# Issuing a batch's load one block later in a two-layer attention kernel

## The chip, the cores and the metric

The kernel runs on one core of a Trainium2 chip. The metric is the device time of one execution in microseconds (us), as a median of several runs. Each core has TensorE (PE in the profile; its weight loads are PEld), VectorE (DVE), ScalarE (ACT), GpSimd (POOL) and SyncE (SP). SyncE here only issues DMAs.

## The reference

The input x is 16 batches of 256 channels by 32 x 32 positions, in float32. Two layers are applied, each of the form x = x + attention(gn(x)):

```
def _L0_conv_ref(x, Wq, bq, Wk, bk, Wv, bv, rel_h, rel_w):
    ...                                   # b = 16, heads = 4, d = 64, n = 1024
    q = proj(Wq, bq)
    k = proj(Wk, bk)
    v = proj(Wv, bv)
    sim = jnp.einsum('bhdi,bhdj->bhij', q, k)
    rel = (rel_h + rel_w).reshape(heads, d, n)
    qpos = jnp.einsum('hdi,bhdj->bhij', rel, q)
    attn = jax.nn.softmax(sim + qpos, axis=-1)
    out = jnp.einsum('bhdn,bhmn->bhdm', v, attn)

x = x + _L0_conv_ref(_gn(x), ...)
x = x + _L1_conv_ref(_gn(x), ...)
```

`_gn` takes, for each batch, the mean and variance over all channels, all rows and a group of two columns (16 groups), and normalizes with them.

## The kernel before, in words

A *unit* is one batch in one layer: `units` holds 32 pairs (b, l) in the order (0,0), (1,0), (2,0), (0,1), (3,0), (1,1), (4,0), (2,1) and so on, so that from unit 3 on the odd units are second layers and the even ones first layers, until the batches run out. A unit has four *blocks*: a pair of heads (pr = 0 or 1) by a half of the 512 query positions (half = 0 or 1). Block b = 0..3 of unit u is (u, b // 2, b % 2). The loop `for n in range(len(blocks)): block(n)` (L712) writes out all 128 blocks, and the order of the code is the order of the instructions on each engine. Engines meet only by semaphores.

In a block, for each of eight stretches j of 128 key positions, VectorE writes the position term into PSUM (`seed`, L332), TensorE adds the product of k and q to it (`scores`, L348), ScalarE takes the exponential into a tile p (L357), and VectorE adds the p's up for the denominators (`add_up`, L366 and L368). TensorE then multiplies p with v (`attend`, L382). Between these stand the projections of the next heads or the next unit (`project` L251, `values` L281, `positions` L309), and the group norm of units further ahead: sums of x by ScalarE (L176) for unit u + 2 start near the end of block 0 of unit u, `norm_squares` follows in block 2, `norm_apply` (L231) one unit later.

The denominators take a way over DRAM. After each second block (half = 1) TensorE sums the p's over the partitions (`sums_of_p`, L405), and ScalarE copies products and sums out of PSUM to the tile od (`take_out`, L422). Then four small DMAs bring the sums into `den_all` (L431). In the next block (half = 0) `reciprocals` takes 1/x on VectorE (L439), writes it to DRAM (rd, two DMAs, L442) and reads it back, broadcast over 64 partitions (rden, two DMAs of 256 KB, L445). At the end of that block `finish` multiplies with it (L456), adds bias and x (L457), and in the second layer writes the result out (L459, 512 KB):

```
for h in range(2):
    nc.sync.dma_start(
        rdens[u, pr][h * D : (h + 1) * D],
        rd[h : h + 1].to_broadcast([D, 2, HALF]),
    )
```

After finish VectorE still has an `add_up` and the seeds for j = 1, 2, 3 of the next block before it, and then, in that next block, the last additions of the block before and the seed for j = 4.

All these DMAs are issued by SyncE, and so are the loads of x (L101, two DMAs of 512 KB for a batch). The first three batches are loaded ahead of the loop, the other 13 in it, by `load_x`, during unit u for the batch of unit u + 3:

```
def load_x(b):
    xt[b] = xpool.tile([P, CC, N], F32, tag="x", name=f"x_{b}")
    for cc in range(CC):
        nc.sync.dma_start(xt[b][:, cc, :], flat(x[b, cc * P : (cc + 1) * P]))
```

`units[u + 3][0] not in xt` is true in the odd units 1, 3, ..., 25. The pool of x has five tiles, used in turn.

Of the kernel before, what the change touches and what calls it, by code (L numbers as in the profile page):

```python
# [52 lines left out]
def fast_path(ctx, tc, sh, x, layers, out, W, den_all, token):  # L53
# [42 lines left out]
    xt = {}  # L96
# [5 lines that stand above are left out]
# [26 lines left out]
    units = [(b, 0) for b in range(3)]  # L128
# [3 lines left out]
    NU = len(units)  # L132
# [47 lines left out]
    def norm_sums(u, gs):  # L180
        if u not in reds:
            reds[u] = small.tile([P, G], F32, tag="red", name=f"red_{u}")
        for g in gs:
            of_group(u, g, AF.Identity, reds[u])
# [26 lines left out]
    def norm_squares(u, gs):  # L211
        for g in gs:
            of_group(u, g, AF.Square, sums[u], bias=negs[u][:, g : g + 1])
# [14 lines left out]
    def norm_apply(u, gs):  # L228
        rstd, shift = rss[u]
        for g in gs:  # L230
            nc.scalar.activation(  # L231
                grouped(xns[u], g),
                grouped(xt[units[u][0]], g),
                AF.Identity,
                bias=shift[:, g : g + 1],
                scale=rstd[:, g : g + 1],
            )
# [89 lines left out]
    def seed(blk, j, tag):  # L327

        u, pr, half = blk
        ps = psum2(tag, f"ps_{u}_{pr}_{half}_{j}")  # L330
        ab = abt[u, pr][:, :, j, :]
        nc.vector.tensor_tensor(  # L332
            ps.rearrange("p h (w y) -> p h w y", y=H),
            ab[:, :, :H].unsqueeze(2).to_broadcast([P, 2, XH, H]),
            ab[:, :, H + half * XH : H + (half + 1) * XH]
            .unsqueeze(3)
            .to_broadcast([P, 2, XH, H]),
            ALU.add,
        )
        seeds[blk, j] = ps  # L340

    def scores(blk, j):
        u, pr, half = blk
        ps = seeds.pop((blk, j))
        for h, hs in enumerate(QUARTERS):
            for x, c in enumerate(QUARTERS):
                j0 = j * P + x * D
                nc.tensor.matmul(  # L348
                    ps[c, h, :],
                    ks[u, pr][hs, j0 : j0 + D],  # L350
                    qs[u, pr][hs, half * HALF : (half + 1) * HALF],
                    start=False,
                    stop=True,
                    skip_group_check=True,
                )
        p = ppool.tile([P, 2, HALF], F32, tag="p", name=f"p_{u}_{pr}_{half}_{j}")
        nc.scalar.activation(p, ps, AF.Exp, bias=W.shift)  # L357
        probs[blk, j] = p

    def add_up(blk, j):  # L360
        u, pr, half = blk
        if j == 0:
            return
        if j == 1:
            accs[blk] = apool.tile([P, 2, HALF], F32, tag="acc", name=f"acc_{u}_{pr}_{half}")
            nc.vector.tensor_tensor(accs[blk], probs[blk, 0], probs[blk, 1], ALU.add)  # L366
        else:
            nc.vector.tensor_tensor(accs[blk], accs[blk], probs[blk, j], ALU.add)  # L368
# [66 lines left out]
    def reciprocals(u, pr):  # L435

        n = index[u, pr, 0]
        r8 = fpool.tile([P, 2, 8], F32, tag="r8", name=f"r8_{u}_{pr}")
        nc.vector.reciprocal(r8, den_all[:, n : n + 2, :])  # L439
        rd = dpool.tile([2, 2, HALF], F32, tag="rd", name=f"rd_{u}_{pr}")  # L440
        for x in range(2):
            nc.sync.dma_start(rd[:, x, :].rearrange("h (a b) -> h a b", b=8), r8[:, x, :])  # L442
        rdens[u, pr] = opool.tile([P, 2, HALF], F32, tag="rden", name=f"rden_{u}_{pr}")
# [5 lines that stand above are left out]
# [23 lines left out]
    def prepare(u, b):  # L472

        x, y = ring[3], ring[2]
        if b == 0:
            return (
                values(u, 1, psum2(x, f"pv_{u}_1")),
                project(u, 1, "q", psum2(y, f"pq_{u}_1")),
            )
        if b == 1:  # L480
            return (
                project(u, 1, "k", psum2(x, f"pk_{u}_1")),
                positions(u, 1, psum2(y, f"pa_{u}_1")),
            )
        u += 1
        if u == NU:
            return (nothing, nothing), (nothing, nothing)
        if b == 2:
            return (
                project(u, 0, "q", psum2(x, f"pq_{u}_0")),  # L490
                project(u, 0, "k", psum2(y, f"pk_{u}_0")),
            )
        return (
            values(u, 0, psum2(x, f"pv_{u}_0")),
            positions(u, 0, psum2(y, f"pa_{u}_0")),
        )

    def block(n):
        blk = blocks[n]
        u, b = divmod(n, BPU)  # L500
        half = blk[2]
        before = blocks[n - 2][:2] if half == 0 and n > 0 else None
        after = blocks[n + 1] if n + 1 < len(blocks) else None
        one, two = u + 1 < NU, u + 2 < NU

        pieces = u + 1 < NU or b < 2
        f0, f1, f2, f3 = ring

        if half == 1:
            add_up(blocks[n - 1], 7)  # L510
        for j in range(1, 4):
            scores(blk, j)
        if b == 2 and u + 3 < NU and units[u + 3][0] not in xt:
            load_x(units[u + 3][0])
        (first, first_out), (second, second_out) = prepare(u, b)
        first(0)
        if b == 0 and one:
            norm_apply(u + 1, range(0, 1))
        if b == 1 and two:
            norm_sums(u + 2, range(9, 11))  # L520
        seed(blk, 4, f1)
        scores(blk, 4)
        add_up(blk, 1)
        if half == 0:
            if before:
                reciprocals(*before)
            add_up(blk, 2)
        if b == 0 and one:
            norm_apply(u + 1, range(1, 5))
        if b == 1 and two:  # L530
            norm_sums(u + 2, range(11, 12))
        if b == 2 and two:
            norm_squares(u + 2, range(0, 5))
        second(0)
        if half == 1:
            second_out()
        first(1)
        first_out()
        seed(blk, 5, f0)
        scores(blk, 5)  # L540
        if half == 0:
            add_up(blk, 3)
            second(1)
            second_out()
        seed(blk, 6, f1)
        scores(blk, 6)
        if pieces and half == 0:
            ring[2:] = f3, f2
        seed(blk, 7, ring[2])
        scores(blk, 7)  # L550
        if half == 1:
            add_up(blk, 2)
            add_up(blk, 3)
        add_up(blk, 4)

        if after:
            seed(after, 0, f0)
        if before:
            finish(*before)
        if b == 0 and one:  # L560
            norm_apply(u + 1, range(5, 9))
        if b == 0 and two:
            norm_sums(u + 2, range(0, 2))
        if b == 1 and two:
            norm_sums(u + 2, range(12, G))
        if b == 1 and one:
            norm_apply(u + 1, range(9, 11))
        if b == 2 and two:
            norm_squares(u + 2, range(5, 11))
        po = psum2(ring[3], f"po_{n}")  # L570
        values_of_p = attend(blk, po)
        values_of_p(0)
        if two and half == 1:
            mean, mean_out = (norm_mean if b == 1 else norm_var)(u + 2, zeroed(f1, f"pm_{n}"))
            mean(0)
        if after:
            scores(after, 0)
        if two and half == 1:
            mean(1)
            values_of_p.word()  # L580
            mean_out()
        add_up(blk, 5)
        if half == 1:
            add_up(blk, 6)
            add_up(blk, 7)
        if after:
            for j in range(1, 4):
                seed(after, j, ring[j % 3])
        if half == 0:
            add_up(blk, 6)  # L590
        if b == 0 and two:
            norm_sums(u + 2, range(2, 9))
        if b == 1 and one:
            norm_apply(u + 1, range(11, G))
        if b == 2 and two:
            norm_squares(u + 2, range(11, G))
        values_of_p(1)
        if half == 1:
            sums_of_p(blocks[n - 1 : n + 1], po)
        take_out(blk, po)  # L600
# [410 lines left out]
```

## Time and profile before

| | |
|---|---|
| median of 3 runs | 2654.65 us (2654.4 to 2658.43) |
| profiled execution | 2655.58 us |
| its span, first to last instruction | 2652.5 us |
| granted clock of TensorE, mean | 0.995 |
| busy: TensorE, VectorE, ScalarE, GpSimd | 98%, 91%, 75%, 7% of the span |
| DMA: moved, mean rate | 75.48 MB, 28 GB/s |
| largest kinds of DMA | rden 128 x 256 KB, x 32 x 512 KB, output 32 x 512 KB |

A profile's row of a group reads: line, engine, operation, output<-inputs, count, and times. A timeline's row gives the start in us from the span's beginning, the duration, engine and line, what it writes and reads, how many instructions were merged, and in brackets how long the engine had been idle before it and what ended that. An arrow in the waits points from the one who waited to the one who released it. For DMAs the row tells of the issue on SyncE's queue (SPq), not of the transfer.

### The profile page before, as it was taken

The numbers are of one execution on the slowest core, as the hardware profiler recorded it, in microseconds if no ns is written. First come the engines' busy times: TensorE is split into PE (matmuls) and PEld (weight loads), VectorE is DVE, ScalarE is ACT, GpSimd is POOL, SyncE is SP. The second block draws the span as 40 slices with busy tenths as digits, with TensorE's granted clock in tenths as the row PEclk, the third lists the DMA queues.
The fourth block names the chain that finished last, engine by engine and source line by source line (L and its number), as shares of the span: only waits on it lengthen the run. The fifth ranks groups of instructions, "written<-read, shape, count | busy, mean of one in ns | idle before, by whom it ended". The sixth has DMA issues, their size and how long they took to land.

```text
span 2652.5 us, 86141 instructions
## 1 busy us (share of the span) xinstructions
PE 2591.0 (98%) x38406; PEld 1389.7 (52%) x38406; DVE 2423.2 (91%) x2198; ACT 1980.2 (75%) x3916; POOL 176.5 (7%) x450
## 2 busy tenths in 40 slices
PE   7999999999999999999999999999999999999994
PEld 3555555555555555555555555555555555555552
DVE  6999999999999999999999999999999999999996
ACT  5778777787777787777877777877778777778652
POOL 1000000000000000000000000000000000000000
PEclk9999999999999999999999999999999999999997
DMA  2010010101001010010100101001010100000001
GB/s 74 11 33 18 26 34 19 34 26 34 26 19 42 18 42 18 18 50 10 42 26 10 50 18 34 26 26 34 19 34 27 34 26 19 26 18 26 26 26 34
DMA packets 61499, 75.48 MB, mean 28 GB/s; under 512 B 43200, under 2 KB 44736, under 8 KB 61120
## 3 DMA queue, kind: packets, MB, share of 16 engines
q1 hardware_dynamic: 59664, 69.83, 9.1%
q8 instruction: 302, 4.95, 0.8%
q14 instruction: 77, 0.63, 0.1%
q10 hardware_dynamic: 1456, 0.07, 0.0%
HBM read 52.04 MB, written 17.30 MB: 26 GB/s over the span
## 4 chain that ended last, share of the span: by engine, by line
PE 84%; DVE 6%; DMA 6%; SPq 2%; issue 1%; ACT 1%; POOL 0%; DVEq 0%; POOLq 0%
PE po L382 30%; PE ps L348 29%; PE pv L281 7%; PE pq L251 7%; PE pk L251 7%; DVE ps L332 3%; PE po L405 2%; DMA rd<-r 2%; DMA rden<-rd 2%; PE pa L309 2%; DVE acc L368 2%; DMA den_all<-od 1%; SPq L431 1%; DVE x L457 1%; DVE od L456 1%
## 5 line engine op out<-in xcount | busy, mean ns | idle before, releaser
L357 ACT ACTIVATE p<-ps,shift 128x1024 f32<-128x1024 f32 x1024 | 1092.3, 1114 | 337.4 <-PE ps L348 215.4
L332 DVE TENSOR_TENSOR ps<-abt 128x1024 f32<-128x1024 f32 x1024 | 1228.7, 1228 | 112.3 <-ACT p L357 94.1
L348 PE MATMUL ps<-q,k 64*64 64x512 f32 x8192 | 997.5, 593 | 15.5 <-DVE ps L332 15.1
L368 DVE TENSOR_TENSOR acc<-acc,p 128x1024 f32<-128x1024 f32 x768 | 933.7, 1216 | 16.1 <-DVE r L439 0.2
L382 PE MATMUL po<-p,v 64*64 64x256 f32 x16384 | 933.1, 376 | 0.3 <-POOL token L152 0.3
L382 PEld LDWEIGHTS po<-p,v 64*64 64x64 f32 x16384 | 668.3, 133 | 294.6 <-issue 60.4
L348 PEld LDWEIGHTS ps<-q,k 64*64 64x64 f32 x8192 | 299.1, 133 | 443.3 <-issue 273.3
L251 PE MATMUL pq<-xn,Wq 64*64 64x512 f32 x2048 | 244.3, 592 | 4.0 <-DVE xn L640 4.0
L281 PE MATMUL pv<-Wv,xn 64*64 64x256 f32 x4096 | 244.3, 376 | 1.6 <-POOL token L152 1.3
L251 PE MATMUL pk<-xn,Wk 64*64 64x512 f32 x2048 | 242.8, 589 | 0.0
L231 ACT ACTIVATE xn<-x,nshift,rstd 128x128 f32<-128x128 f32 x501 | 213.4, 501 | 1.6 <-POOL nshift L654 1.6
L281 PEld LDWEIGHTS pv<-Wv,xn 64*64 64x64 f32 x4096 | 153.6, 133 | 103.3 <-issue 51.1
L176 ACT ACTIVATE junk<-x,neg 128x128 f32<-128x128 f32 x489 | 191.7, 399 | 0.0
L152 POOL MEMSET token<- 1x1 f32 x380 | 33.8, 89 | 2360.2 <-PE po L382 657.9
L422 ACT COPY od<-po 128x1024 f32<-128x1024 f32 x64 | 64.8, 1012 | 152.1 <-PE po L405 152.1
L366 DVE TENSOR_TENSOR acc<-p,p 128x1024 f32<-128x1024 f32 x128 | 155.9, 1218 | 0.0
L251 PEld LDWEIGHTS pq<-xn,Wq 64*64 64x64 f32 x2048 | 78.5, 134 | 145.6 <-issue 133.0
L176 ACT ACTIVATE junk<-x 128x128 f32<-128x128 f32 x480 | 144.9, 311 | 0.7 <-DVE x L457 0.7
L251 PEld LDWEIGHTS pk<-xn,Wk 64*64 64x64 f32 x2048 | 75.4, 133 | 124.2 <-issue 124.2
L220 POOL TENSOR_TENSOR rstd<-var,mhalf 128x16 f32<-128x16 f32 x30 | 113.2, 3773 | 59.1 <-ACT var L218 59.1
L456 DVE TENSOR_TENSOR od<-od,rden 128x1024 f32<-128x1024 f32 x64 | 78.2, 1221 | 31.9 <-DMA rden<-rd 31.8
L291 ACT COPY v<-pv 128x1024 f32<-128x1024 f32 x64 | 64.8, 1012 | 48.1 <-PE pv L281 48.1
(59 smaller groups left out, 921.1 us busy)
## 6 DMA issues: line engine op xcount, KB each, us to landing
rden<-rd SPq DMA_DIRECT2D x128, 256.0 KB
x<-in_x_dram SPq DMA_DIRECT2D x32, 512.0 KB
out_dram<-x SPq DMA_DIRECT2D x32, 512.0 KB
den_all<-od SPq DMA_DIRECT2D x256, 2.0 KB
rd<-r SPq DMA_DIRECT2D x128, 4.0 KB
raw<-in_L_conv_Wq_dram SPq DMA_DIRECT2D x2, 256.0 KB
raw<-in_L_conv_Wk_dram SPq DMA_DIRECT2D x2, 256.0 KB
raw<-in_L_conv_Wv_dram SPq DMA_DIRECT2D x2, 256.0 KB
```

The source lines that it names most:

```text
L176: nc.scalar.activation(junk, grouped(xt[units[u][0]], g), func, accum_out=into[:, g : g + 1], **bias)
L220: nc.gpsimd.tensor_tensor(rstd, var, W.mhalf[:, :G], ALU.pow)
L231: nc.scalar.activation(grouped(xns[u], g), grouped(xt[units[u][0]], g), AF.Identity, bias=shift[:, g : g + 1], scale=rstd[:, g : g + 1],)
L251: yield nc.tensor.matmul(pk[c, nh, :], w[l][rs, cc, c0 : c0 + D], xns[u][rs, cc, nh * HALF : (nh + 1) * HALF], start=(t == 0 and cc == 0), ...
L281: yield nc.tensor.matmul(pv[c, a, i, :], xns[u][rs, cc, j0 : j0 + D], W.wv[l][rs, cc, :], start=(t == 0 and cc == 0 and i == 0), stop=(t = ...
L332: nc.vector.tensor_tensor(ps.rearrange("p h (w y) -> p h w y", y=H), ab[:, :, :H].unsqueeze(2).to_broadcast([P, 2, XH, H]), ab[:, :, H + h ...
L348: nc.tensor.matmul(ps[c, h, :], ks[u, pr][hs, j0 : j0 + D], qs[u, pr][hs, half * HALF : (half + 1) * HALF], start=False, stop=True, skip_g ...
L357: nc.scalar.activation(p, ps, AF.Exp, bias=W.shift)
L366: nc.vector.tensor_tensor(accs[blk], probs[blk, 0], probs[blk, 1], ALU.add)
L368: nc.vector.tensor_tensor(accs[blk], accs[blk], probs[blk, j], ALU.add)
L382: yield nc.tensor.matmul(po[c, a, :QUART], vts[u][rs, j, c0 : c0 + D], p[rs, h, a * QUART : (a + 1) * QUART], start=(t == 0 and j == 0), s ...
L456: nc.vector.tensor_tensor(o, o, rden, ALU.mult)
```

## The change

The condition under which `load_x` is called in `block` names block 3 in place of block 2. The call stands at the same place in the block: behind the scores for j = 1, 2, 3, ahead of the projections.

```
         for j in range(1, 4):
             scores(blk, j)
-        if b == 2 and u + 3 < NU and units[u + 3][0] not in xt:
+        if b == 3 and u + 3 < NU and units[u + 3][0] not in xt:
             load_x(units[u + 3][0])
```

In block 2 that place lies ahead of the call of `reciprocals` (L526) and of `finish` (L559), both of which are made in blocks 0 and 2; in block 3 neither is called.

More of the change, by code (lines that the diff above doesn't have):

```diff
@@ L512, in block @@
             scores(blk, j)
-        if b == 2 and u + 3 < NU and units[u + 3][0] not in xt:
+        if b == 3 and u + 3 < NU and units[u + 3][0] not in xt:
             load_x(units[u + 3][0])
```

## Prediction

> **What bounds the kernel now.** I read the page first, for the busy shares and the chain that ended last, then the waits, and then the timelines of single engines in three stretches of two blocks.
>
> ```profile
> span 2652.5 us, 86141 instructions
> PE 2591.0 (98%) x38406; PEld 1389.7 (52%) x38406; DVE 2423.2 (91%) x2198; ACT 1980.2 (75%) x3916; POOL 176.5 (7%) x450
> PE 84%; DVE 6%; DMA 6%; SPq 2%; issue 1%; ACT 1%; POOL 0%; DVEq 0%; POOLq 0%
> ```
>
> TensorE sets the time. A change that only moves a transfer can gain no more than TensorE now loses around it. But the chain has 6% of DMA in it, so somewhere the path runs through transfers. The waits say which one (waiting engine and line, releaser: total us, times, longest):
>
> ```profile
> DVE od L456 <- DMA rden<-rd: 31.8, 19, 7.8
> PE ps L348 <- DVE ps L332: 15.1, 19, 2.7
> ```
>
> VectorE waits in finish (L456) for the broadcast reciprocals, and TensorE waits for a seed that VectorE writes (L332), as often. The 7.8 us is the last finish of the program, behind which nothing is left to do; 24.0 us lie in the other 18. SyncE's timeline (start, duration) shows what goes ahead of the reciprocals. First blocks 2 and 3 of unit 3, which has a load; then the same blocks of unit 27, which also writes its output (L459) but has no load:
>
> ```profile
> 324.61 2.43 SPq L431 DMA_DIRECT2D den_all<-od  x4
> 327.07 1.07 SPq L101 DMA_DIRECT2D x<-in_x_dram  x2
> 328.62 1.12 SPq L442 DMA_DIRECT2D rd<-r  x2
> 333.80 1.14 SPq L445 DMA_DIRECT2D rden<-rd  x2
> 341.29 0.34 SPq L459 DMA_DIRECT2D out_dram<-x  x1
> ```
>
> ```profile
> 2267.37 2.42 SPq L431 DMA_DIRECT2D den_all<-od  x4
> 2271.36 1.12 SPq L442 DMA_DIRECT2D rd<-r  x2
> 2274.42 1.14 SPq L445 DMA_DIRECT2D rden<-rd  x2
> 2282.21 0.34 SPq L459 DMA_DIRECT2D out_dram<-x  x1
> ```
>
> From issue of rd to issue of rden (which waits for rd to land) it is 333.80 - 328.62 = 5.18 us with a load and 2274.42 - 2271.36 = 3.06 without. Over all pairs of blocks I find 4.95 to 5.56 in the 13 with a load, and a mean of 3.06 in the others. The load's packets of 4 KB run from 1.2 to 4.8 us after its issue, and the small packets of rd end 0.4 to 0.8 us later: rd queues behind 1 MB. VectorE's timelines, unit 3 and then unit 27:
>
> ```profile
> 338.71 1.23 DVE L456 TENSOR_TENSOR od<-od,rden 128x1024 f32<-128x1024 f32 x1 [1.75 <-DMA rden<-rd]
> ```
>
> ```profile
> 2279.64 1.22 DVE L456 TENSOR_TENSOR od<-od,rden 128x1024 f32<-128x1024 f32 x1
> ```
>
> And ScalarE's copy L422 ends every second block, so its starts are the clock of a pair of blocks (unit 3, unit 27):
>
> ```profile
> 323.57 1.01 ACT L422 COPY od<-po 128x1024 f32<-128x1024 f32 x1 [1.34 <-PE po L405]
> ...
> 364.72 1.01 ACT L422 COPY od<-po 128x1024 f32<-128x1024 f32 x1 [3.23 <-PE po L405]
> ```
>
> ```profile
> 2266.33 1.01 ACT L422 COPY od<-po 128x1024 f32<-128x1024 f32 x1 [1.34 <-PE po L405]
> ...
> 2306.46 1.01 ACT L422 COPY od<-po 128x1024 f32<-128x1024 f32 x1 [3.23 <-PE po L405]
> ```
>
> With the load the pair takes 364.72 - 323.57 = 41.15 us, without it 40.13. Finish starts 338.71 - 323.57 = 15.14 us after the copy, against 2279.64 - 2266.33 = 13.31. So 1.83 us of delay on VectorE became 1.02 us on the path: 0.8 us was slack. TensorE's timeline shows where it bites, at the scores for the fourth block's j = 4:
>
> ```profile
> 349.39 1.09 PE L348 MATMUL ps<-q,k 64*64 64x512 f32 x8 [0.72 <-DVE ps L332]
> ```
>
> **The change, step by step.** Nothing is added or taken out. Two DMA instructions on SyncE's queue (512 KB each) move, 13 times, past four others, rd, rd, rden, rden, and in 12 of the 13 also past the output's write (L459), whose unit is of the second layer. ScalarE, VectorE, TensorE and GpSimd keep their order.
>
> *What goes away.* All 13 pairs have the pattern above. Their lengths over 40.13 are, in order of time, 0.93, 1.02, 1.22, 0.70, 1.00, 0.72, 1.51, 1.25, 1.10, 1.55, 1.44, 0.96 and 1.06 us: 14.46 us in sum. From unit 2 to unit 29 the same blocks of units without a load take 40.13 each (one 40.17), the other pairs (blocks 0 and 1) 40.25 or 40.26, also right after a load, so nothing of the loss is caught up later. In each of the 13 the excess is the start of finish less 14.1 us, within 0.03: 14.1 is the point from which TensorE feels it. Without the load ahead of it rd lands 2.04 us sooner (5.10 - 3.06, the two means), and finish, now at 15.24 in the mean, falls back to 13.2, where VectorE's own work holds it. The other pairs from unit 2 on start finish between 13.2 and 14.02 us, with one at 14.45 near the end, since den_all sometimes lands up to 1.6 us late; that stays. So I take the whole 14.46 us. What is late next is TensorE itself: the load-free pair is 40.13 us of work with no wait in its matmuls.
>
> *Where the load goes.* SyncE runs ahead of the blocks: it issues what its own waits let through. The load, which waits for nothing (SyncE's waits name no instruction of L101), will go out right behind L459, some 16 us after the copy (17.7 now, less the delay of finish), in unit 1 right behind rden. It lands some 6 us after that (1.2 us to start, the output's packets of 1.5 us ahead of it, 3.6 us of its own), so about 23 us after the copy. Behind it on the queue stand the four den_all of the next copy, 41 us after this one: 18 us free. The tile's slot was left by the write of a unit whose last finish lies six blocks back, 120 us.
>
> *What it could cost there.* First its reader: the sums of x at L176 start in the next unit's first block, for unit 3's load at 380.62, which is 57 us after the copy, so 34 us of lead remain of 49 (the load now lands 3.5 + 4.8 us after the copy). [...] By the rows, early issue is what costs 1.11 us a load, and the lead left is over five times what the load takes; I go by the rows. Secondly, in unit 1 only, the load starts on the heels of rden (256 KB twice). The nearest row is the load on the heels of den_all now: the reciprocal behind den_all starts 5.01 us after the copy with a load and 5.08 without, so no loss, and no gain to be had there either. I take 0; at worst rden is late by the load's 3.6 us, and finish at 13.0 + 3.6 passes the 14.1 by 2.5 us, once. Thirdly, 1.5 MB in a row (output and load) replaces 1.5 MB nearly in a row (load and rden) some 12 us earlier, for the other users of the DMA engines, the instruction fetches. I take 0 and keep 0 to 0.2 us a load. A gain beyond 14.46 would have to come from the pair falling below 40.13, which no load-free pair does.
>
> **Sum.** The profiled execution took 2655.58 us (span 2652.5), 0.93 above the median and inside the three runs: 2655.58 - 14.46 = 2641.1, span 2638.0. On the median: 2654.65 - 14.46 = 2640.2 us, 0.54% faster.
>
> **Rivals.** *No change* (0.05): the load pairs are long for what the load does to the core while it lands, not for its place, or the finish isn't what TensorE waits for. Then they stay at 41.24 and the time at 2654.65. For it: TensorE's named wait is only 15.1 us in all. Against: the 0.03 us fit with the start of finish.
>
> *Half* (0.07): the load behind the output disturbs something in the fourth block, at some 0.5 us a load; 14.46 - 13 x 0.5 = 8.0 us gained, 2646.7. VectorE has the least room there, 0.8 us. Against: between finish and the next den_all no compute instruction waits for a transfer.
>
> *Slower* (0.04): instruction fetches. The page has 302 of them, 16 KB each, so one every 2652 / 302 = 8.8 us, and in the fourth block one may stand behind output and load for up to 6 us. It decides from the point where TensorE stands still for more than 1.11 us a load; [...] a fetch would fall into 6 / 8.8 of the 13 loads and wait 3 us in the mean: 13 x 0.68 x 3 = 27 us, so 2640.2 + 27 = 2667. Against: in the 13 load trains of now, 7 fetches fall within 6 us of the load's issue; they take 0.9 to 1.8 us against a median of 1.0, with no loss beyond finish's. [...]
>
> **How the numbers follow.** The likeliest case, the loss gone with up to 2.5 + 2.6 us of the unknown costs and a run's scatter of some 2 us, has 0.84: 2638 to 2646. That holds 8 in 10, and the range stays there. Within 0.2% (5.3 us) is about what a measurement of this kernel can tell from no change. Faster by more: the likeliest and the half, 0.91; within: 0.05; slower: 0.04.
>
> **What would show it.** Right: rd to rden 3.1 us in all pairs, L101 after L459 on SyncE, VectorE's wait at L456 down from 31.8 to about 9 us, all pairs of blocks 2 and 3 at 40.13, DMA gone from the chain in the middle. Wrong: finish at 13.3 and pairs still over 40.13, with a new releaser at L348; L176 waiting for x; rden late in unit 1.

## The result, and the profile after

The changed kernel took 2646.12 us (median of 6 runs, 2643.18 to 2647.72), the kernel before 2656.38 us (6 runs, 2653.53 to 2660.8): a ratio of 0.9958, 95% interval 0.9945 to 0.9971. The forecast was 2640.2 us and a ratio of 0.9946. Direction and mechanism came as forecast; the gain in the medians is 10.3 us in place of 14.5.

The page of the changed kernel, span, busy shares and the chain by engine:

```profile
span 2643.5 us, 86127 instructions
PE 2589.6 (98%) x38406; PEld 1394.9 (53%) x38406; DVE 2422.9 (92%) x2198; ACT 1979.9 (75%) x3916; POOL 175.3 (7%) x450
PE 96%; issue 1%; DVE 1%; DMA 1%; POOL 0%; ACT 0%; SPq 0%; DVEq 0%; POOLq 0%
```

TensorE does the same work, but the path that ended last is now 96% TensorE (84% before), and the transfers have gone from it (1%, before 6%). The two waits that the prediction named (total us, times, longest):

```profile
DVE od L456 <- DMA rden<-rd: 8.5, 4, 7.6
PE ps L348 <- DVE ps L332: 7.1, 7, 2.7
```

7.6 of the 8.5 us are the last finish of the program; in the loop 0.9 us is left of the 24.0. SyncE's timeline for blocks 2 and 3 of unit 3, the stretch shown for before:

```profile
326.04 2.41 SPq L431 DMA_DIRECT2D den_all<-od  x4
330.02 1.12 SPq L442 DMA_DIRECT2D rd<-r  x2
333.07 1.14 SPq L445 DMA_DIRECT2D rden<-rd  x2
340.87 0.35 SPq L459 DMA_DIRECT2D out_dram<-x  x1
341.27 1.26 SPq L101 DMA_DIRECT2D x<-in_x_dram  x2
```

From rd to rden it is now 333.07 - 330.02 = 3.05 us (5.18 before), and the load goes out right behind the output, 16.3 us after the copy L422, though the block in whose code it stands begins later. In VectorE's timeline the bracket behind finish is gone, and in ScalarE's the copies that bound the pair of blocks are 40.13 us apart (41.15 before):

```profile
338.31 1.22 DVE L456 TENSOR_TENSOR od<-od,rden 128x1024 f32<-128x1024 f32 x1
```

```profile
325.00 1.01 ACT L422 COPY od<-po 128x1024 f32<-128x1024 f32 x1 [1.33 <-PE po L405]
...
365.13 1.01 ACT L422 COPY od<-po 128x1024 f32<-128x1024 f32 x1 [3.23 <-PE po L405]
```

All 13 pairs together have 0.07 us of excess over 40.13, where before had 14.46. So 14.4 us went, and yet the spans differ by 2652.5 - 2643.5 = 9.0 only. The rest was lost again in three places, found by comparing the starts of the same copies in the two profiles: 2.4 us up to the first copy (83.75 in place of 81.36), 1.2 us in the pairs without a load, and 1.9 us in the last pair of blocks (39.67 in place of 37.81).

In the last pair it is TensorE's clock, granted at 0.50 and 0.52 in the stretches below. The rows are a stretch of before and then of after; the columns are the stretch, its length, busy us (and instructions) of TensorE, weight loads, VectorE, ScalarE and GpSimd, granted clock, DMA share, GB/s:

```profile
2595.00:2598.00 3.00, 2.71 (x16) 0.31 (x9) 3.00 (x4) 1.11 (x1) 0.00 (x0) 0.50 0.39 111
```

```profile
2585.00:2592.00 7.00, 5.85 (x44) 2.44 (x48) 6.96 (x7) 3.34 (x3) 0.00 (x0) 0.52 0.29 77
```

In the 5 us ahead of these stretches TensorE is busy for only 1.5 and 2.2, as there is no next unit to project, and then its granted clock stands at half: for 3.41 us in the profile of before and for 6.83 us, twice as long, in that of after, by the clock's records. At half rate, by my estimate, the 3.41 us more are worth up to 3.41 / 2 = 1.7 of the 1.9 us. What sets these lengths was not shown. At the start TensorE was slow for longer too, in projections in whose rows no wait stands; before, then after:

```profile
28.14 1.89 PE L251 MATMUL pk<-xn,Wk 64*64 64x512 f32 x16
```

```profile
29.38 3.05 PE L251 MATMUL pk<-xn,Wk 64*64 64x512 f32 x16
```

The same 16 matmuls take 3.05 in place of 1.89 us; in block 2 of unit 3 of before, at full clock, they take 1.90. The clock's records begin, at full, at 27.91 us in the profile of before and at 31.70 in that of after; of the time ahead of that they say nothing. If the rate was half up to there, the second row lost (31.70 - 29.38) / 2 = 1.16 us, and 3.05 - 1.16 = 1.89. The same working holds in all 14 profiles of this document: in each the first copy comes 54.95 or 54.96 us after the start of the first projection plus half of the time from that start to the first record. By this estimate 1.4 of the 2.4 us at the start are half rate: (31.70 - 25.91) / 2 - (27.91 - 24.90) / 2. The other 1.0 us is the first projection itself, which began at 25.91 us and not at 24.90; ahead of it, in the profile of after, TensorE waited 0.54 us for the weights Wv.

In the pairs without a load, the cause stands in two rows of the worst one, which is one of blocks 0 and 1:

```profile
773.45 0.25 DVE L439 RECIPROCAL r<-den_all 128x16 f32<-128x16 f32 x1 [1.85 <-DMA den_all<-od]
```

```profile
775.97 1.09 PE L348 MATMUL ps<-q,k 64*64 64x512 f32 x8 [0.21 <-DVE ps L332]
```

den_all landed late, the reciprocal held VectorE's queue, and TensorE waited for the seed behind it (0.21 us stand as idle, the pair lost 0.44). None of the three places lies in code that the change touches. Whether they are the change's doing or chance was the first question for the experiments.

### The profile page after: what moved, and what is told of

It reads as the page before. It is cut to its first block, busy times and chain, and to the rows that moved or that the text cites. A ratio compares the mean times of both kernels' runs of the same rounds, so it can differ in the third digit from the quotient of the medians.

```text
span 2643.5 us, 86127 instructions
## 1 busy us (share of the span) xinstructions
PE 2589.6 (98%) x38406; PEld 1394.9 (53%) x38406; DVE 2422.9 (92%) x2198; ACT 1979.9 (75%) x3916; POOL 175.3 (7%) x450
## 4 chain that ended last, share of the span: by engine, by line
PE 96%; issue 1%; DVE 1%; DMA 1%; POOL 0%; ACT 0%; SPq 0%; DVEq 0%; POOLq 0%
PE po L382 34%; PE ps L348 33%; PE pk L251 8%; PE pv L281 8%; PE pq L251 8%; PE po L405 2%; PE pa L309 2%; PE pm L196 0%; DMA den_all<-od 0%; DVE ps L332 0%; SPq L431 0%; POOL rstd L652 0%; DVE acc L368 0%; ACT od L422 0%; DMA rden<-rd 0%
## 5 line engine op out<-in xcount | busy, mean ns | idle before, releaser
L422 ACT COPY od<-po 128x1024 f32<-128x1024 f32 x64 | 64.8, 1012 | 152.2 <-PE po L405 152.2
L262 ACT ACTIVATE q<-pq,bq 128x1024 f32<-128x1024 f32 x64 | 71.4, 1116 | 39.4 <-PE pq L251 39.4
```

The lines of the kernel that those rows point to most:

```text
L262: nc.scalar.activation(t.rearrange("p (a n) -> p a n", a=NH), pk, AF.Identity, bias=bias[l][:, pr : pr + 1])
```

## The experiments

**Is it chance?** Each kernel once more, unaltered. First the changed one:

> The changed kernel once more, unaltered, for more executions and a second profile. Theory A (the load ahead of rd cost 14.4 us and nothing replaces it; the first comparison came out smaller, 10.3 us, since 2.4 us at the start and 1.9 us at the end of the profiled execution came from TensorE's half clock lasting longer, and 1.1 us from den_all landing late by chance): the pairs of blocks 2 and 3 are 40.13 us again, start and end differ from the first profile by some us, and the medians differ by 10 to 15 us. Theory B (the new place costs some 0.3 us a load): the median gain stays at 10 us and the same pairs are over 40.13 or 40.25 as in the first profile.

Measured: 2644.49 us against 2657.18 for before in the same series, ratio 0.9954 (0.9941 to 0.9968), 12.7 us. In its profile the 13 pairs have 0.10 us of excess, the start is 82.69, the last pair 37.79, with a granted clock of 0.99, 0.50 and 0.97 in the 5, 3 and 5 us from 2578 on, so some 3.4 us at half. Then the kernel before:

> The kernel before, unaltered, for a second profile. Theory A (the first profile of before was a favourable one: start 81.36 us to the first copy L422, 0.16 us of excess outside the load pairs, one half-clock window of 3.41 us ahead of the end): the load pairs lose 14.4 us again, within 1 us, while start, the other pairs and the end are some 2 us worse in sum, as in the profiles of the changed kernel. Theory B (the changed kernel itself has the worse start, end and other pairs): the second profile of before repeats 81.4, 0.2 and one window.

Measured: 2659.63 us, ratio to the earlier runs of before 1.0003 (0.9994 to 1.0011). Its second profile has 12.73 us of excess in the load pairs (under the 13.4 that theory A allowed), a start of 83.73, a last pair of 39.61 with 6.83 us of half clock, and 0.8 us of excess in the other pairs: in sum start, end and other pairs are 4.8 us worse than in its first profile, where theory A had some 2. So the slow end belongs to neither kernel: each showed both forms. The slow start doesn't belong to the changed one either: 81.36 and 83.73 before, 83.75 and 82.69 after, and 82.31 to 83.93 in the other ten profiles. The 81.36 of the first profile, from which the forecast was made, came only once. Over both profiles of each, the spans differ by (2652.5 + 2655.5) / 2 - (2643.5 + 2640.6) / 2 = 12.0 us. For the excess outside the load pairs theory A holds less well: 0.2 and 0.8 us before, 1.3 and 1.5 us after. That stays open.

**Does the new place cost anything?** A second load behind each one, into a tile that nothing reads:

```
+    def load_more(b):
+        more = xpool.tile([P, CC, N], F32, tag="more", name=f"more_{b}", bufs=1)
+        for cc in range(CC):
+            nc.sync.dma_start(more[:, cc, :], flat(x[b, cc * P : (cc + 1) * P]))
...
             load_x(units[u + 3][0])
+            load_more(units[u + 3][0])
```

> The changed kernel, and behind each of the 13 loads in block 3 a second load of 1 MB into a tile that nothing reads. Theory A (the new place is free, 18 us of room): no difference from the changed kernel, 2644 to 2648. Theory B (a cost of 0.3 us a load in the new place, by instruction fetches or by what the load does while it lands): 4 us more than the changed kernel, 2650.

Measured: 2645.07 us, ratio 0.9952 (0.9938 to 0.9965), against 2644.49 of the changed kernel in the same series. SyncE's queue and ScalarE's copies around unit 3's load:

```profile
339.74 0.35 SPq L464 DMA_DIRECT2D out_dram<-x  x1
340.14 1.26 SPq L101 DMA_DIRECT2D x<-in_x_dram  x2
341.45 0.94 SPq L106 DMA_DIRECT2D more<-in_x_dram  x2
365.04 1.14 SPq L436 DMA_DIRECT2D den_all<-od  x2
```

```profile
323.87 1.01 ACT L427 COPY od<-po 128x1024 f32<-128x1024 f32 x1 [1.33 <-PE po L410]
...
364.00 1.01 ACT L427 COPY od<-po 128x1024 f32<-128x1024 f32 x1 [3.22 <-PE po L410]
```

40.13 us with 2 MB there, and no excess in the sum of the 13 pairs. Theory B (0.3 us a load) falls: the new place is free.

**The same doubling in the old place**, by the same edit in the kernel before:

> The kernel before, and behind each of the 13 loads in block 2 a second load of 1 MB into a tile that nothing reads: 2 MB ahead of rd. Theory A (rd queues behind the load's bytes; the excess of a pair is the start of finish less 14.1 us): rd to rden 5.1 + about 3 us, finish at 18 to 19 us, 4 to 4.8 us of excess a pair, 40 to 48 us more than before, some 2697 to 2705. Rival (the load slows the core while it lands): the excess doubles at most, 2657 + 14 = 2671.

Measured: 2697.09 us, 37.5 over before (2659.59), ratio 1.0143 (1.0127 to 1.0158). SyncE's queue and finish in unit 3:

```profile
333.04 1.06 SPq L101 DMA_DIRECT2D x<-in_x_dram  x2
334.14 0.91 SPq L106 DMA_DIRECT2D more<-in_x_dram  x2
335.15 1.81 SPq L447 DMA_DIRECT2D rd<-r  x2
342.05 1.16 SPq L450 DMA_DIRECT2D rden<-rd  x2
```

```profile
346.82 1.22 DVE L461 TENSOR_TENSOR od<-od,rden 128x1024 f32<-128x1024 f32 x1 [3.89 <-DMA rden<-rd]
```

rd to rden takes 342.05 - 335.15 = 6.9 us, in the mean of the 13 pairs too, and finish starts at 17.97 in the mean. The rule "excess is the start of finish less 14.1" gives 13 x 3.87 = 50.3 us for these pairs; they have 50.66. The absolute time fell into theory A's range; the difference from before, 37.5, stayed just under its 40 to 48, since rd went out later behind the added issues (6.21 us after the copy in the mean, 5.29 before) and so waited for less. The rival's doubling, 14 us, is far off. The same second load cost 50.66 - 14.46 = 36 us in one place and nothing in the other.

**Half of the bytes** ahead of rd:

```
-        if b == 2 and u + 3 < NU and units[u + 3][0] not in xt:
-            load_x(units[u + 3][0])
+        if b == 2 and u + 3 < NU and units[u + 3][0] not in xt:
+            load_x(units[u + 3][0], [0])
+            rest.append(units[u + 3][0])
+        if b == 3 and rest:
+            load_x(rest.pop(), [1])
```

> The load in halves: the first DMA of 512 KB in block 2 ahead of rd, the second in block 3. Theory A (a threshold: 0.9 us of slack between 13.2 and 14.1): 512 KB take 1.8 us of DMA time and delay rd by some 0.2 us, so no loss but where den_all is late; as the changed kernel, 2644 to 2648. Rival (loss in proportion to the bytes ahead of rd): half of the loss stays, 7 us, about 2652.

Measured: 2645.26 us, ratio 0.9946 (0.9932 to 0.9959). A threshold, then: 512 KB cost nearly nothing. The size of the delay was off: rd to rden is 3.89 us in the mean, 0.83 over the free case and not 0.2. Finish comes at 13.99, just inside the slack, and 1.55 of the 1.59 us of excess lie in two pairs where den_all was late as well.

**Is it block 2, or the place in the queue?** Load in block 2, but behind the reciprocals (the call in block 3 is gone):

```
             if before:
                 reciprocals(*before)
+                if b == 2 and u + 3 < NU and units[u + 3][0] not in xt:
+                    load_x(units[u + 3][0])
```

> Load in block 2 as before, but called behind the reciprocals, so behind rd and rden on SyncE's queue. Theory A (only the place ahead of rd counts): rd to rden 3.1 us, finish at 13.2 to 14.1, time as the changed kernel within 3 us, some 2644 to 2648. Rival (a load anywhere in block 2 disturbs it, or on the heels of rden delays rden): pairs with a load stay at 41.2, time as before, 2656.

Measured: 2646.3 us, ratio 0.9954 (0.994 to 0.9968), rd to rden 3.06. And the load one block *earlier* than before (`b == 1`):

> Load one block earlier than before, in block 1, so that it goes out behind the rden of block 0, 20 us sooner. Theory A: as the changed kernel, 2644 to 2648, since it isn't the lateness but the wait behind which the load stands that counts. Rival (it is the later issue that helps): as before or slower, 2656 or more.

Measured: 2644.87 us, ratio 0.9948 (0.9934 to 0.9961). Later, same block or earlier: all are as good as the changed kernel. In both the load goes out on the heels of rden, 13 times, and in the pairs with it finish stays at 13.6 and 13.7 us in the mean; the few pairs over 40.13 (blocks 2 and 3) or 40.25 (blocks 0 and 1) by more than 0.1 us are those where den_all was late.

**Would another queue do?** The load in block 2 as before, issued by ScalarE:

```
-    def load_x(b):
+    def load_x(b, queue=nc.sync):
...
-            nc.sync.dma_start(xt[b][:, cc, :], flat(x[b, cc * P : (cc + 1) * P]))
+            queue.dma_start(xt[b][:, cc, :], flat(x[b, cc * P : (cc + 1) * P]))
...
-            load_x(units[u + 3][0])
+            load_x(units[u + 3][0], nc.scalar)
```

> The load in block 2 as before, but issued by ScalarE, so on another queue than rd. Theory Q (order on SyncE's queue is what holds rd back): rd's packets get between the load's, rd to rden 3.1 to 3.8 us, little loss, 2645 to 2650, with up to 1.3 us a load of ScalarE's time for two issues. Theory E (the 16 DMA engines shared are what holds it back, whichever queue): rd to rden stays near 5 us and the time as before, 2655 to 2658.

Measured: 2665.31 us, slower than before by 5.7 us, ratio 1.0022 (1.0015 to 1.0029). Neither theory had this. ScalarE's queue and SyncE's in unit 3, and VectorE's reciprocal:

```profile
328.20 0.34 ACTq L101 DMA_DIRECT2D x<-in_x_dram  x1
...
328.57 0.44 ACTq L101 DMA_DIRECT2D x<-in_x_dram  x1
```

```profile
326.49 2.41 SPq L431 DMA_DIRECT2D den_all<-od  x4
332.45 1.12 SPq L442 DMA_DIRECT2D rd<-r  x2
335.51 1.14 SPq L445 DMA_DIRECT2D rden<-rd  x2
```

```profile
332.17 0.25 DVE L439 RECIPROCAL r<-den_all 128x16 f32<-128x16 f32 x1 [2.18 <-DMA den_all<-od]
```

rd to rden is 3.06, as theory Q said, but not for its reason: rd comes after the load has passed. ScalarE issues the load at 328.20, 0.7 us sooner than SyncE could (which has den_all's four issues to do first, up to 326.49 + 2.41 = 328.90), and so it meets den_all, which is on SyncE's queue. The reciprocal starts at 7.29 us in the mean of the 13 pairs (5.01 before), finish at 15.52, and the pairs lose 20.6 us. The packets show the meeting: the last one of den_all ends 6.50 us after the copy in these pairs and 4.55 in the pairs without a load, though the load's packets are on a queue of their own. So such a queue gave no shelter here. That fits theory E's reason, only with another victim; what the two transfers share was not shown.

**The consumer's side.** If the load costs only by way of finish, a finish with more slack must make the old place harmless. First `finish` behind all three seeds for the next block, by the same edit in the changed kernel and in the one before:

```
-        if before:
-            finish(*before)
...
             for j in range(1, 4):
                 seed(after, j, ring[j % 3])
+        if before:
+            finish(*before)
```

> The changed kernel with finish called behind the three seeds of the next block instead of ahead of them. Theory (what is left of waits between VectorE and TensorE in the loop is the 1 to 1.5 us a run where den_all lands late by an instruction fetch and finish passes 14.1): these go too, all pairs 40.13 and 40.25, 1 to 1.5 us less than the changed kernel. Rival (the later finish delays something else: the additions, the tile od, the output): slower than the changed kernel by a few us.

> The kernel before, load ahead of rd in block 2, with finish called behind the three seeds of the next block. Theory A (the load costs time only by way of rden, finish and the seeds behind finish): rd to rden stays at 5.1 us, but TensorE no longer waits, the load pairs are 40.13, time as the changed kernel, 11 to 14 us under before. Rival (the load's bytes beside the blocks, or a wait other than finish's, cost the time): as before.

Measured: 2711.6 and 2710.73 us, ratios 1.0195 (1.0181 to 1.0209) and 1.0192 (1.0178 to 1.0206). Both forecasts of the time failed, for a reason that has nothing to do with the load. In the changed kernel's variant:

```profile
351.10 1.23 DVE L332 TENSOR_TENSOR ps<-abt 128x1024 f32<-128x1024 f32 x1 [1.69 <-ACT p L357]
352.24 1.22 DVE L456 TENSOR_TENSOR od<-od,rden 128x1024 f32<-128x1024 f32 x1
```

The third seed needs a PSUM tile that ScalarE hasn't read yet. Where finish stood it had filled this 1.69 us. Without it every pair of blocks takes about 1 us longer (41.09). What the two were made for they still show: with the load in the old place the 13 pairs are 41.11 us in the mean and the load-free pairs of the same blocks 41.09.

So finish belongs in that very gap, ahead of the third seed (again its old call is gone):

```
             for j in range(1, 4):
+                if before and j == 3:
+                    finish(*before)
                 seed(after, j, ring[j % 3])
```

> The changed kernel with finish called between the seeds for j = 2 and j = 3 of the next block, so that it fills the 1.69 us in which VectorE waited for ScalarE ahead of the third seed when finish stood behind all three. Theory: finish starts at about 16.7 us, 3.4 us later than rden lands at best, so neither a load nor a late den_all reaches TensorE; pairs 40.13 and 40.25 without exception, 1 to 1.5 us less than the changed kernel, so 0.5% under before. Rival (any delay of the first two seeds' neighbours costs, as behind three seeds): 41.1 a pair, some 2710.

> The kernel before, load ahead of rd in block 2, with finish between the seeds for j = 2 and j = 3 of the next block. Theory A (the load costs time only by way of rden and finish): rd to rden 5.1 us in the 13 pairs, rden lands at about 15.1 us, finish at 16.7 doesn't wait, the pairs are 40.13, time as the one above, within 1 us. Rival: the 13 pairs stay about 1 us longer than the others, 13 us more than the one above.

Measured: 2645.39 us, ratio 0.9951 (0.9937 to 0.9965), with the load in the new place; 2646.48 us, ratio 0.9957 (0.9943 to 0.997), with the load in the old one. In the second, SyncE's queue, finish and the copies of unit 3:

```profile
328.76 1.12 SPq L442 DMA_DIRECT2D rd<-r  x2
334.05 1.15 SPq L445 DMA_DIRECT2D rden<-rd  x2
```

```profile
340.44 1.21 DVE L456 TENSOR_TENSOR od<-od,rden 128x1024 f32<-128x1024 f32 x1
```

```profile
323.73 1.01 ACT L422 COPY od<-po 128x1024 f32<-128x1024 f32 x1 [1.34 <-PE po L405]
...
363.86 1.01 ACT L422 COPY od<-po 128x1024 f32<-128x1024 f32 x1 [3.23 <-PE po L405]
```

rd still stands behind the load for 5.29 us, finish no longer waits, and the pair takes 40.13, as do all 13. The loss can be cured at either end. The two are 1.1 us apart (within 1 was forecast). The forecast of 1 to 1.5 us below the changed kernel failed: 1.8 us of excess outside the load pairs remained with the load in the new place, though finish started 3.3 us later (16.83 in the mean). A late den_all reaches TensorE earlier, by the reciprocal itself, as in the two rows of the result. None of the versions beats the changed kernel by more than a run's scatter.

## Why the prediction was right, and where it was off

*What goes away.* Right. rd to rden is 3.06 us in the 13 pairs, finish at 13.50 in the mean (13.2 forecast), the pairs at 40.13, but one at 40.22. The rule that a pair's excess is the start of finish less 14.1 us held far outside the range from which it was read (doubled load).

*Where the load goes.* Right: 16.3 us after the copy behind L459, in unit 1 behind rden (9.8 us). Its first reader in unit 4 started at 381.04, 56 us after the copy.

*What it costs there.* I took 0 and kept up to 2.5 us for unit 1 and 0.2 us a load for the rest. 0 it is, shown by the doubled load; on the heels of rden the load was harmless in two more kernels, 13 times each. It was not early issue as such that cost 1.11 us a load: earlier (block 1, ratio 0.9948) and later (block 3, 0.9954 in the same series) gave the same. The half and the slower rival fall with the doubled load, the rival of no change with the profile after. The time alone would not have told the half from the forecast: the ratio on the forecast's own median, 0.9958 x 2654.65 = 2643.5 us, lies midway between 2640.2 and the half's 2646.7, and the new median, 2646.12, at the upper edge of the likeliest case's 2638 to 2646, 0.1 us past it.

*Sum.* Off here, by 5.9 us: 1.7 in the median of before and 4.2 in the gain. It took the profile's start, end and load-free pairs as those of any execution, and subtracted one profile's loss from a median of three runs. Three terms were mis-sized. The loss of the 13 pairs was 14.46 us in the first profile and 12.73 in the second. The median of before was 2656.38 with six runs, not 2654.65. And from execution to execution some 2 us of start and 2 us of end come and go (first copy at 81.36 to 83.75, last pair 37.79 to 39.67 in the four profiles of the unaltered kernels), for the most part, by the estimates above, with TensorE's half clock; the profile of before had the short form of both. "A run's scatter of some 2 us" was too little: the six runs of before alone lie 7.3 us apart. The gain by medians was 10.3 us in the first series and 12.7 in the second, and 14.46 lies at the edge of the first one's interval. The room that was kept for costs of the new place, which did not come, took up most of what these terms added: so far the number was luck, the mechanism not.

*Rows forecast.* VectorE's wait at L456 at about 9 us: 8.5. DMA gone from the middle of the chain: yes.

Still open: whether the 0.5 to 1.3 us more of excess outside the load pairs in the two profiles of the changed kernel is systematic. The load's place alone does not sort it: by the same measure the doubled load has 0.8 us in block 3 and 2.2 in block 2.

## What to carry to other kernels

A load that nothing waits for can cost time through a small DMA behind it that someone does wait for, here 14.46 us for 13 loads of 1 MB: look for which wait on the issuing queue lets the load out, and which short round trip starts next. Then price it by the consumer's slack; half of the bytes cost almost nothing here (1.59 us), twice the bytes over three times as much (50.66). And before forecasting half a per cent, compare the start and the end of several profiles, not only the loop.

## What the runs showed of the hardware

Late small transfers go together with instruction fetches. In seven profiles (both kernels twice, the loads behind rden, in block 1 and doubled in block 3) I compared the 60 pairs from the third on. In half of the 420 cases a fetch packet of 16 KB (from the queue that has 302 of them in the page) overlapped the time from 1.0 to 4.8 us after the copy, in which den_all is under way. With one the reciprocal started 5.38 us after the copy in the mean and 6.51 at worst, without one 4.81 and 5.25. Of the 131 starts later than 5.2 us, 129 had such a fetch. This is a coincidence in time, shown in the packets; no run took the fetches away, so the cause isn't shown.

TensorE's half clock stands in the loop too in two kernels whose waits are longer: with 2 MB ahead of rd the records have three stretches of 3.41 us at half clock between 517 and 1835 us, where both unaltered kernels have none before the last unit; the load by ScalarE has one, at 1149 us. The three lie in the three pairs of the doubled load in which the excess is 0.2 to 0.3 us above the start of finish less 14.1; in the other ten the two agree within 0.03.
